# The second batch's attention denominators: repeating transfers through HBM in place of matmuls with a spreading matrix

## The chip, the cores and the metric

One core of a Trainium2 chip runs one program. The metric is device time in microseconds (us), lower is better. The program uses TensorE (PE in the profile; its weight loads are PEld), VectorE (DVE), ScalarE (ACT), GpSimd (POOL) and SyncE (SP), which issues almost all transfers. Everything is float32.

## What is computed

One transformer layer over 2 x 1024 tokens of width 512, on normalized input: linear attention with 16 heads of 32 features beside a gated feed-forward layer with low-rank experts. The part that the change touches is the division in the attention:

```python
Q = jax.nn.elu(Q) + 1.0
K = jax.nn.elu(K) + 1.0
KV = jnp.einsum('bhsd,bhse->bhde', K, V)
QKV = jnp.einsum('bhsd,bhde->bhse', Q, KV)
K_sum = jnp.sum(K, axis=-2)
QK_sum = jnp.einsum('bhsd,bhd->bhs', Q, K_sum)
out = QKV / (QK_sum[..., None] + 1e-08)
```

The kernel divides early: it multiplies each query feature by one over its head's denominator, so that `Q / denominator` can be stored and later be multiplied by `KV` and the output weights together. There is one denominator for each head and token, and 32 features of a head share it. After the attention and the experts the layer adds `x`.

## The kernel before

**Tiling and stages.** Tokens are two batches of 1024, each seen as two halves (`g` 0 and 1) of 512. Keys come first (`k_pair`), then the queries of batch 0 (`query_unit(0)`), its denominators (`denominators(0)`, line 874), the queries of batch 1 (`query_unit(1)`), its denominators, the leftover columns of the gate and up weights for both batches (`rest(0)` and `rest(1)`, line 1053), ten units of the feed-forward layer (`unit(j, b)`, line 1250), and the down projection. Products are split by Strassen's scheme, so between matmuls there are many sums of tokens, of weights and of results.

**Query features.** A batch has eight blocks of features, `qt[b, c, g]`, each 128 features (chunk `c`, four heads) by 512 tokens. Batch 0 has them in eight tiles of a work pool. Batch 1 has them in two slots: slot 4 holds the blocks of `c` 0 and 2, slot 5 those of `c` 1 and 3. Both slots are used again soon: slot 5 for `wi` (`inner_weight_sums`, line 1165, called at line 1491), slot 4 for `ti23_0` (`token_sums_23`, line 1149, called at line 1506).

**Denominators.** Eight matmuls a batch (line 879) gather them in one PSUM tile, 128 rows (four for each of 16 heads and two halves, equal among themselves) by 512 tokens; VectorE adds epsilon and takes the reciprocal into `den` (lines 883 and 884). A row then has to reach the 32 partitions of its head.

- Batch 0: `den` is stored to `d_dram` (line 887) and each block gets a tile `bc` by four transfers, each of which reads one row and writes it to 32 partitions (line 871, `spread_den`), 64 KB each. There are three `bc` buffers (`NBC`): a block's transfers are issued when an earlier multiply has freed one. `attend(0)` multiplies two blocks at a time, at four points of `query_unit(1)`.
- Batch 1: eight matmuls (line 901) with the 0/1 matrix `spread`, which GpSimd builds early (`make_spread`, line 220), put the repeated rows into PSUM banks `pb`. `attend(1, 0)` stands at the end of `rest(0)` and `attend(1, 1)` right after it.

In both, a multiply (line 909) works in place, and a transfer (line 914) stores the block to `q_dram`, 256 KB.

**Order.** On PE, DVE, ACT and POOL the order is the one in which the code calls the instructions. SyncE's order is made by a scheduler when the program is built, and then is fixed. Each engine works in its order and waits in place. Transfers use eight completion counters in turn, so each waits until the one issued eight before it has landed.

**What stands around.** On VectorE, from the reciprocal on: four sums `ti` (line 1135), two rows `hr` (line 1068, the gated product of `rest`), eight additions for the folding of low-rank weights (line 975), an `hr` row, the eight multiplies, eight weight sums of unit 0 (`fold_sums`, lines 979 to 982), four token sums (`token_sums_1`, line 1157), three `hr` rows, four sums `wi` (lines 1179 to 1182), two `hr` rows, and then the first unit. On GpSimd: `xdiff` (line 1013), eight weight sums `w` and `wi2` (line 1179), and without a break four `ti23_0`, four token sums of batch 1, four `ti56_1` and four `ti23_1` (lines 1135 and 1157); after these the two adds `r<-r,r` of the first unit (line 1365, by the helper's line 1287). In a unit, `r<-r,x` (line 1219) and `r<-r,ab` (lines 1233 and 1241) read PSUM halves that TensorE then writes again, and `r<-r,b` (line 1287, called at line 1378) overwrites the tiles that GpSimd's adds read.

```python
    def rest(b, between=(None, None)):        # line 1053
...
    rest(0, (first_fold, lambda: attend(1, 0)))
    attend(1, 1)
    token_diffs(1, "den")
    for i in range(2):
        fold_sums(0, i)
    token_sums_1(nc.vector, 0)
    rest(1, (lambda: list(inner_weight_sums(nc.vector, 0, (1, 5, 6))), None))
```

Of the kernel before, what the change touches and what calls it, by code (L numbers as in the profile page):

```python
# [10 lines left out]
F32 = mybir.dt.float32  # L11
# [4 lines left out]
P = 128  # L16
# [21 lines left out]
def layer_kernel(  # L38
# [23 lines left out]
    nc = tc.nc  # L62
# [26 lines left out]
    SG = P // 32  # L89
# [3 lines left out]
    NPQ = NC // 2  # L93
    WARM = 13, 3
    NBC = 3
# [20 lines left out]
    r_dram = [dram.tile([2, REST, 2, UT], F32, name=f"r_dram{b}") for b in range(NBATCH)]  # L116
    q_dram = [[dram.tile([2, P, 4, UT], F32, name=f"q_dram{b}_{j}") for j in range(NPQ)] for b in range(NBATCH)]
    w_dram = [dram.tile([E, 2 * TPB, P], F32, name=f"w_dram{b}") for b in range(NBATCH)]
    d_dram = dram.tile([P, TB], F32, name="d_dram")
    kvo_dram = [dram.tile([P, NC, D], F32, name=f"kvo_dram{b}") for b in range(NBATCH)]  # L120

    ffn_stack = ExitStack()
# [8 lines left out]
    p2 = pool(p2_stack, "p2")  # L131
    p2w = pool(p2_stack, "p2w", bufs=2)
# [6 lines left out]
    ident = const.tile([P, P], F32, name="ident")  # L139
# [5 lines left out]
    def hold(v):  # L145

        nc.vector.memset(v, 0.0)
# [48 lines left out]
    for b in range(NBATCH):  # L196
        t = p2.tile([P, 2, NC, 32], F32, name=f"ksd{b}")
# [16 lines left out]
    nc.gpsimd.memset(before, 0.0)  # L214
    for e in range(1, E):
        nc.gpsimd.memset(before[:, e, 0:e], 1.0)

    spread = p2.tile([P, 2, P], F32, name="spread")

    def make_spread():  # L220
        for c in range(SG):
            rows = slice(c * 32, (c + 1) * 32)
            for g in range(2):
                nc.gpsimd.tensor_copy(
                    spread[rows, g, :].rearrange("p (h k) -> p h k", k=DK),
                    ident[rows, :]
                    .rearrange("p (c h j) -> p c h j", h=HPC, j=32 // HPC)[:, c, :, 4 * g : 4 * g + 1]
                    .to_broadcast([32, HPC, DK]),
                )

    idle = p1.tile([P, 2], F32, name="idle")
    nc.gpsimd.memset(idle, 0.0)
    mv = p1.tile([P, NTILE, nc.vector.BN_AGGR_DIM], F32, name="mv")
# [442 lines left out]
    for n in range(2):  # L676
# [13 lines left out]
        (2, "n"): [load_factors],  # L690
        (2, "b"): [lambda: load_weights(wv_sb, wvT)],
        (3, "n"): [lambda: next(wq_sums)],
        (3, "b"): [lambda: load_weights(wo_sb, woT), gather_factors, make_spread],
        (4, "n"): [lambda: next(wq_sums), lambda: next(wq_sums)],
        (6, "n"): [lambda: next(wq_sums)],
        (7, "n"): [lambda: pair_token_sums(0)],
# [8 lines left out]
    def load_weights(t, w):  # L705
        hold(t[:, 0, 0:1])
        nc.sync.dma_start(out=t, in_=by_chunk(w))

    late = None
    for m in range(NTILE // 2):  # L710
# [21 lines left out]
        else:  # L732
# [4 lines left out]
            if m == 3:  # L737
                wo_sb = slot(5, [NC, D], "wo_sb")
# [118 lines left out]
            nc.tensor.matmul(pa, agu_sb[:, c, :], xt(b, c, cols), start=(c == 0), stop=(c == NC - 1))  # L857
        nc.vector.tensor_mul(xa[b][:, cols], pa, wT[b][:, cols])

    dens, bcs = {}, {}  # L860

    def spread_den():

        i = len(bcs)
        if i == 2 * NC:
            return
        g, c = divmod(i, NC)
        t = p2w.tile([P, TB], F32, tag=f"bc{i % NBC}", name=f"bc{i}", bufs=1)
        for h in range(HPC):
            row = c * 32 + 8 * h + 4 * g  # L870
            nc.sync.dma_start(out=t[h * DK : (h + 1) * DK, :], in_=d_dram[row, :].partition_broadcast(DK))
        bcs[i] = t

    def denominators(b):

        pd = bank(f"pd{b}")
        for g in range(2):
            for c in range(NC):
                nc.tensor.matmul(
                    pd[c * 32 : (c + 1) * 32, :], ksd[b][:, g, c, :], qt[b, c, g], start=(g == 0), stop=(g == 1)  # L880
                )
        den = ffn.tile([P, TB], F32, tag="den", name=f"den{b}")
        nc.vector.tensor_scalar_add(den, pd, DIV_EPS)
        nc.vector.reciprocal(den, den)
        dens[b] = den
        if b == 0:
            nc.sync.dma_start(out=d_dram, in_=den)
            for i in range(NBC):
                spread_den()

    attended = []

    def attend(b, g=None):

        if b:
            todo = [(c, g) for c in range(NC)]
            by = []
            for c in range(NC):
                rows = slice(c * 32, (c + 1) * 32)
                by.append(bank(f"pb{b}_{g}_{c}"))  # L900
                nc.tensor.matmul(by[c], spread[rows, g, :], dens[b][rows, :], start=True, stop=True)
        else:
            k = len(attended)
            attended.extend((k, k + 1))
            todo = [(i % NC, i // NC) for i in attended[-2:]]
            by = [bcs[i] for i in attended[-2:]]
        for (c, g), t in zip(todo, by):
            v = qt[b, c, g]
            nc.vector.tensor_mul(v, v, t)
            if b == 0:  # L910
                spread_den()

            j, i = c % NPQ, c // NPQ
            nc.sync.dma_start(
                out=q_dram[b][j][:, :, 2 * i + g, :].rearrange("s p n -> p s n"),
                in_=v.rearrange("p (s n) -> p s n", n=UT),
            )

# [134 lines left out]
    def rest(b, between=(None, None)):  # L1053
        t, _, bd = w_rest
        spare = [f"qt{k}{g}" for k in range(NC) for g in range(2)]
        blk = [ts(g, TB) for g in range(2)]

        def gated_rows(ps, first, n, g, dst):

            h, v = (  # L1060
                p2w.tile([P, TB], F32, tag=spare.pop(0), name=f"{n_}{b}_{g}_{dst.start}", bufs=1) for n_ in ("hr", "ur")
            )
            gr, ur = slice(first, first + n), slice(first + n, first + 2 * n)
            nc.scalar.activation(h[gr, :], ps[gr, :], AF.Silu)
# [12 lines left out]
        halves = [ps[2 * RB * g : 2 * RB * (g + 1), :] for g in range(2)]  # L1077
        for g in range(2):
            nc.tensor.matmul(halves[g], bd[:, P:], xa[b][:, blk[g]], start=True, stop=False, skip_group_check=True)
        for k in range(NC):  # L1080
            for g in range(2):
                nc.tensor.matmul(
                    halves[g], t[:, k, P:], xt(b, k, blk[g]), start=False, stop=(k == NC - 1), skip_group_check=True
                )
        flush()
        for g in range(2):
            gated_rows(ps, 2 * RB * g, RB, g, slice(RA, REST))
        for g in range(2):
            ps = bank(f"pr{b}_{g}")
            nc.tensor.matmul(ps, bd[:, 0:P], xa[b][:, blk[g]], start=True, stop=False)  # L1090
            for k in range(NC):
                nc.tensor.matmul(ps, t[:, k, 0:P], xt(b, k, blk[g]), start=False, stop=(k == NC - 1))  # L1092
            flush()
            gated_rows(ps, 0, RA, g, slice(0, RA))
            if between[g]:
                between[g]()
# [56 lines left out]
    def token_sums_1(eng, b):  # L1153

        t = xnT[b][0][:, :, TB:BT].rearrange("p k (h n) -> p k h n", n=TH)
        b11, b21 = tsum[b][1][:, 0], tsum[b][1][:, 1]
        eng.tensor_sub(t[:, 0, 0], b11[:, TH:], b11[:, 0:TH])
        eng.tensor_sub(t[:, 0, 1], b21[:, TH:], t[:, 0, 0])
        eng.tensor_sub(t[:, 1, 0], b21[:, TH:], b11[:, TH:])
        eng.tensor_sub(t[:, 1, 1], b21[:, 0:TH], t[:, 0, 1])  # L1160
        inner_tokens(b, (1,), lambda i, k: t[:, k // 2, k % 2])
# [320 lines left out]
        for i in range(2):  # L1482
            fold_adds(0, i, pf)

    rest(0, (first_fold, lambda: attend(1, 0)))
    attend(1, 1)
    token_diffs(1, "den")
    for i in range(2):
        fold_sums(0, i)
    token_sums_1(nc.vector, 0)  # L1490
    rest(1, (lambda: list(inner_weight_sums(nc.vector, 0, (1, 5, 6))), None))
    flush()
    ps8.close()
    p2_stack.close()
# [683 lines left out]
```

## Time and profile before

| | |
|---|---|
| median of three runs | 722.59 us (722.54 to 722.98) |
| the profiled execution's own time | 722.83 us |
| its span in the profile | 721.0 us, 9901 instructions |
| TensorE busy | 714.4 us (99%), 3426 matmuls |
| VectorE busy | 578.4 us (80%) |
| ScalarE, GpSimd busy | 198.3 us (28%), 142.6 us (20%) |
| `pb` matmuls (16 passes of 0.587 us, overlapping) | from 222.9 to 225.4 us |
| multiplies of batch 0, of batch 1 | 0.687 and 0.680 us each |
| `bc` transfers of batch 0 | 32, issued from 179.9 to 201.3 us |
| `TensorE` clock granted | 1.00 |

Times in the profile are counted from the start of its span. A row of a timeline gives the start, the time until the last of the row's instructions ends, the engine, the line, the operation, output and inputs by name, how many (`x8`), and in brackets how long the engine had been idle just before and what ended that. A matmul in float32 takes two or more passes, and so a row can say `x16` for eight matmuls. `SPq` rows are the issue of a transfer on SyncE, not its landing. The chain of waits gives start, length and what the path went through.

### The profile page before, as it was taken

The numbers are of one execution on the slowest core, as the hardware profiler recorded it, in microseconds if no ns is written. First come the engines' busy times: TensorE is split into PE (matmuls) and PEld (weight loads), VectorE is DVE, ScalarE is ACT, GpSimd is POOL, SyncE is SP. The second block draws the span as 40 slices with busy tenths as digits, with TensorE's granted clock in tenths as the row PEclk, the third lists the DMA queues.
The fourth block names the chain that finished last, engine by engine and source line by source line (L and its number), as shares of the span: only waits on it lengthen the run. The fifth ranks groups of instructions, "written<-read, shape, count | busy, mean of one in ns | idle before, by whom it ended". The sixth has DMA issues, their size and how long they took to land.

```text
span 721.0 us, 9901 instructions
## 1 busy us (share of the span) xinstructions
PE 714.4 (99%) x3426; PEld 491.4 (68%) x3426; DVE 578.4 (80%) x1327; ACT 198.3 (28%) x438; POOL 142.6 (20%) x176
## 2 busy tenths in 40 slices
PE   8999999999999999999999999999999999999998
PEld 6666676454434566566566566566688899899897
DVE  7788767777688678778778778878988889998884
ACT  3534413453532333333333333333200000000000
POOL 4033011101001752211211311544520100000000
PEclk9999999999999999999999999999999999999999
DMA  5243001214475101211211201334662444433101
GB/s 174 103 129 112 1 0 42 57 34 134 128 204 171 30 27 35 89 48 44 89 38 51 87 32 58 117 127 136 205 193 107 128 156 126 146 120 110 59 16 45
DMA packets 61734, 66.85 MB, mean 93 GB/s; under 512 B 10866, under 2 KB 49522, under 8 KB 61428
## 3 DMA queue, kind: packets, MB, share of 16 engines
q1 hardware_dynamic: 61154, 66.20, 29.9%
q8 instruction: 27, 0.44, 0.3%
q14 instruction: 23, 0.19, 0.1%
q10 hardware_dynamic: 530, 0.02, 0.0%
HBM read 44.11 MB, written 22.09 MB: 92 GB/s over the span
## 4 chain that ended last, share of the span: by engine, by line
PE 85%; DVE 12%; ACT 2%; issue 1%; POOL 0%; DVEq 0%; POOLq 0%
PE ab L1205 16%; PE b L1265 8%; PE po L1953 7%; PE pg L410 5%; PE pqu L778 4%; PE pya L1782 4%; PE pxa L1782 4%; PE pyb L1782 3%; PE ph L1650 3%; PE x L1205 3%; PE pxb L1782 2%; PE pyc L1782 2%; PE pxa L857 2%; PE b L1260 2%; PE pqv L778 2%; PE pr L1092 2%
## 5 line engine op out<-in xcount | busy, mean ns | idle before, releaser
L1265 PE MATMUL b<-t,w 128*128 128x512 f32 x160 | 83.2, 601 | 0.1
L410 PE MATMUL pg<-kt,xn 128*128 128x512 f32 x128 | 58.7, 594 | 0.5 <-DVE kt L354 0.5
L1287 POOL TENSOR_TENSOR r<-r,r 128x512 f32<-128x512 f32 x20 | 30.1, 1524 | 85.2 <-DVE t L1287 83.0
L1205 PE MATMUL ab<-ti,wi 128*128 128x256 f32 x180 | 45.4, 379 | 0.0
L1205 PEld LDWEIGHTS ab<-ti,w 128*128 128x128 f32 x140 | 25.1, 189 | 29.5 <-DVE r L1233 8.2
L1287 DVE TENSOR_TENSOR r<-r,r 128x512 f32<-128x512 f32 x60 | 43.2, 762 | 0.0
L1205 PEld LDWEIGHTS ab<-ti,wi 128*128 128x128 f32 x180 | 34.2, 190 | 13.2 <-issue 4.8
L1205 PE MATMUL ab<-ti,w 128*128 128x256 f32 x140 | 41.2, 387 | 0.5 <-DVE r L1233 0.2
L410 PEld LDWEIGHTS pg<-kt,xn 128*128 128x128 f32 x128 | 23.1, 190 | 22.6 <-issue 20.6
L1233 DVE TENSOR_TENSOR r<-r,ab 128x256 f32<-128x256 f32 x50 | 20.9, 419 | 21.6 <-ACT r L1230 21.1
L1238 ACT COPY r<-ab 128x256 f32<-128x256 f32 x50 | 18.6, 373 | 71.1 <-PE ab L1205 71.1
L1265 PEld LDWEIGHTS b<-t,w 128*128 128x128 f32 x160 | 29.2, 190 | 10.6 <-issue 5.9
L1241 DVE TENSOR_TENSOR r<-r,ab 128x256 f32<-128x256 f32 x50 | 20.9, 419 | 16.2 <-ACT r L1238 15.9
L1215 ACT COPY r<-ab 128x256 f32<-128x256 f32 x50 | 18.7, 374 | 48.4 <-PE ab L1205 47.1
L1953 PE MATMUL po<-wd,f 128*128 128x256 f32 x140 | 30.9, 380 | 0.1
L419 POOL TENSOR_TENSOR ksum<-ksum,kt 128x512 f32<-128x512 f32 x12 | 15.8, 1318 | 71.4 <-DVE lg L456 42.4
L1226 ACT COPY r<-ab 128x256 f32<-128x256 f32 x50 | 18.6, 373 | 40.7 <-PE ab L1205 40.7
L1896 DVE TENSOR_TENSOR f<-f 128x256 f32<-128x256 f32 x84 | 29.4, 423 | 0.1
L1953 PEld LDWEIGHTS po<-wd,f 128*128 128x128 f32 x140 | 26.4, 190 | 4.4 <-issue 0.9
L1205 PE MATMUL ab<-xnT,w 128*128 128x256 f32 x100 | 29.4, 390 | 0.0
L1205 PE MATMUL ab<-xnT,wi 128*128 128x256 f32 x100 | 28.1, 379 | 0.0
L1205 PEld LDWEIGHTS ab<-xnT,w 128*128 128x128 f32 x100 | 18.1, 189 | 10.9 <-issue 4.5
(483 smaller groups left out, 1652.1 us busy)
## 6 DMA issues: line engine op xcount, KB each, us to landing
h_dram<-h SPq DMA_DIRECT2D x40, 256.0 KB
f<-h_dram SPq DMA_DIRECT2D x10, 512.0 KB
x_ring<-in_x_dram SPq DMA_DIRECT2D x16, 256.0 KB
q_dram<-qt SPq DMA_DIRECT2D x16, 256.0 KB
xr<-in_x_dram SPq DMA_DIRECT2D x16, 256.0 KB
out_dram<-xr SPq DMA_DIRECT2D x15, 256.0 KB
w<-in_w_gate_dram SPq DMA_DIRECT2D x10, 256.0 KB
w<-in_w_up_dram SPq DMA_DIRECT2D x10, 256.0 KB
```

Source lines behind the costliest of these rows:

```text
L410: nc.tensor.matmul(pg[m], xns[n][:, ts(m, P)], kt, start=(j == 0), stop=(j == TPBATCH - 1))
L778: nc.tensor.matmul(banks[c], wqs[p][:, k, ts(c, P)], tsum[b][p][:, k, :], start=(start and k == 0), stop=(k == 1), skip_group_check=True,)
L1205: nc.tensor.matmul(out, w, t, start=start, stop=True, skip_group_check=True)
L1215: nc.scalar.copy(self.r[0][:, H0], self.ua)
L1233: nc.vector.tensor_add(self.r[1][:, H1], self.r[1][:, H1], self.lo)
L1241: nc.vector.tensor_add(self.r[1][:, H0], self.r[1][:, H0], self.lo)
L1265: nc.tensor.matmul(pb[m], ws[m][:, A_OF[p], ts(k, P)], tsum[b][p][:, k, :], start=start, stop=True, skip_group_check=True)
L1287: eng.tensor_add(to[m], t[m], v[m])
L1650: nc.tensor.matmul(phs[u][g * ER : (g + 1) * ER, :], a, f[:, g, :], start=(ns[0] == 0 and n == 0), stop=(last and n == len(chunks) - 1), s ...
L1782: nc.tensor.matmul(o, lhsT, rhs, start=first, stop=True, skip_group_check=True)
L1896: op(t[:, at, :], t[:, x_, :], t[:, y, :])
L1953: nc.tensor.matmul(ps[p][:, q, :], lhsT, rhs, start=start, stop=stop, skip_group_check=True)
```

## The change

Batch 1 gets its denominators as batch 0 does: `den` is stored to a `d_dram` of its own, and each block's `bc` tile comes by four repeating transfers. `spread`, `make_spread` and the eight matmuls into `pb` are gone. `CHUNKS` gives batch 1 an order of blocks of its own: the four of slot 5 (`c` 1 and 3, both halves), then the four of slot 4. `attend(1)` handles two blocks a call, at four places: two calls after the token sums that follow `rest(0)`, one in the middle of `rest(1)`, one at its end. `fold_sums` moves up into `rest(0)`, and the `wi` sums move from the first to the second place in `rest(1)`.

```diff
-    d_dram = dram.tile([P, TB], F32, name="d_dram")
+    d_dram = [dram.tile([P, TB], F32, name=f"d_dram{b}") for b in range(NBATCH)]
...
-        (3, "b"): [lambda: load_weights(wo_sb, woT), gather_factors, make_spread],
+        (3, "b"): [lambda: load_weights(wo_sb, woT), gather_factors],
...
-    dens, bcs = {}, {}
-    def spread_den():
-        i = len(bcs)
-        if i == 2 * NC:
-            return
-        g, c = divmod(i, NC)
-        t = p2w.tile([P, TB], F32, tag=f"bc{i % NBC}", name=f"bc{i}", bufs=1)
+    CHUNKS = [[(c, g) for g in range(2) for c in range(NC)], [(c, g) for j in (1, 0) for g in range(2) for c in (j, j + NPQ)]]
+    bcs = []
+    def spread_den(b, i):
+        if i >= 2 * NC:
+            return
+        c, g = CHUNKS[b][i]
+        t = p2w.tile([P, TB], F32, tag=f"bc{i % NBC}", name=f"bc{b}_{i}", bufs=1)
         for h in range(HPC):
             row = c * 32 + 8 * h + 4 * g
-            nc.sync.dma_start(out=t[h * DK : (h + 1) * DK, :], in_=d_dram[row, :].partition_broadcast(DK))
-        bcs[i] = t
+            nc.sync.dma_start(out=t[h * DK : (h + 1) * DK, :], in_=d_dram[b][row, :].partition_broadcast(DK))
+        bcs.append(t)
...
-        dens[b] = den
-        if b == 0:
-            nc.sync.dma_start(out=d_dram, in_=den)
-            for i in range(NBC):
-                spread_den()
+        nc.sync.dma_start(out=d_dram[b], in_=den)
+        attended.append(0)
+        for i in range(NBC):
+            spread_den(b, i)
...
-    def attend(b, g=None):
-        if b:
-            todo = [(c, g) for c in range(NC)]
-            by = []
-            for c in range(NC):
-                rows = slice(c * 32, (c + 1) * 32)
-                by.append(bank(f"pb{b}_{g}_{c}"))
-                nc.tensor.matmul(by[c], spread[rows, g, :], dens[b][rows, :], start=True, stop=True)
...
+    def attend(b):
+        for _ in range(2):
+            i = attended[b]
+            attended[b] += 1
+            c, g = CHUNKS[b][i]
             v = qt[b, c, g]
-            nc.vector.tensor_mul(v, v, t)
-            if b == 0:
-                spread_den()
+            nc.vector.tensor_mul(v, v, bcs.pop(0))
+            spread_den(b, i + NBC)
...
-    rest(0, (first_fold, lambda: attend(1, 0)))
-    attend(1, 1)
+    rest(0, (first_fold, lambda: [fold_sums(0, i) for i in range(2)]))
+    token_sums_1(nc.vector, 0)
+    attend(1)
+    attend(1)
     token_diffs(1, "den")
-    for i in range(2):
-        fold_sums(0, i)
-    token_sums_1(nc.vector, 0)
-    rest(1, (lambda: list(inner_weight_sums(nc.vector, 0, (1, 5, 6))), None))
+    rest(1, (lambda: attend(1), lambda: list(inner_weight_sums(nc.vector, 0, (1, 5, 6)))))
+    attend(1)
     flush()
```

In the built program this gives the following orders (blocks and their repeats numbered 0 to 7 in `CHUNKS[1]`).

- VectorE, after the folding additions and an `hr` row: eight weight sums, four token sums, multiplies 0 to 3, three `hr` rows, multiplies 4 and 5, an `hr` row, four `wi` sums, multiplies 6 and 7, an `hr` row, the first unit.
- SyncE, after the weight loads of units 0 and 1: the store of `den`, repeats 0 to 2, three stores to `r_dram`, repeat 3, store 0, repeat 4, store 1, repeat 5, store 2, repeat 6, store 3, three stores to `r_dram`, repeat 7, stores 4 and 5, a store to `r_dram`, stores 6 and 7, a store to `r_dram`, and then sixteen loads `sb`.
- TensorE: the same without `pb`. ScalarE: the same. GpSimd: the same without the eight copies of `make_spread`.
- Waits of the built program that concern this: repeat n (from 3 on) for multiply n - 3; the first `wi` for stores 0 to 3; `ti23_0` for stores 4 to 7; ScalarE's last `hr` row for the last of batch 0's stores to `r_dram`.

More of the change, by code (lines that the diff above doesn't have):

```diff
@@ L216, in layer_kernel @@
         nc.gpsimd.memset(before[:, e, 0:e], 1.0)
-    spread = p2.tile([P, 2, P], F32, name="spread")
-    def make_spread():
-        for c in range(SG):
-            rows = slice(c * 32, (c + 1) * 32)
[L223 to L229, printed above, removed]
     idle = p1.tile([P, 2], F32, name="idle")
@@ L884, in denominators @@
         nc.vector.reciprocal(den, den)
-        dens[b] = den
-        if b == 0:
-            nc.sync.dma_start(out=d_dram, in_=den)
-            for i in range(NBC):
-                spread_den()
-    attended = []
-    def attend(b, g=None):
-        if b:
-            todo = [(c, g) for c in range(NC)]
-            by = []
-            for c in range(NC):
-                rows = slice(c * 32, (c + 1) * 32)
-                by.append(bank(f"pb{b}_{g}_{c}"))
[L901 to L907, printed above, removed]
+        nc.sync.dma_start(out=d_dram[b], in_=den)
+        attended.append(0)
+        for i in range(NBC):
+            spread_den(b, i)
+    attended = []
+    def attend(b):
[3 more added lines that the diff above has]
+            c, g = CHUNKS[b][i]
             v = qt[b, c, g]
-            nc.vector.tensor_mul(v, v, t)
-            if b == 0:
-                spread_den()
-            j, i = c % NPQ, c // NPQ
+            nc.vector.tensor_mul(v, v, bcs.pop(0))
+            spread_den(b, i + NBC)
+            j, k = c % NPQ, c // NPQ
             nc.sync.dma_start(
-                out=q_dram[b][j][:, :, 2 * i + g, :].rearrange("s p n -> p s n"),
+                out=q_dram[b][j][:, :, 2 * k + g, :].rearrange("s p n -> p s n"),
                 in_=v.rearrange("p (s n) -> p s n", n=UT),
```

## The prediction

> All times are microseconds on the axis of the profiled run before. "Block n" (0 to 7) is the second batch's n-th piece of query features, "repeat n" the four transfers that bring its denominators, "multiply n" and "store n" its DVE instruction and its way to q_dram.
>
> **What bounds the kernel.** I read engine totals first (TensorE 714.4 of 721.0), then the chain of waits around the second batch's division, which gives what removing matmuls can be worth:
>
> ```profile
> 219.52 3.43 PE pr L1092 x8
> 222.96 2.41 PE pb L901 x15
> 225.36 1.01 PE pr L1079 x4
> ...
> 249.96 0.68 PE pf L966 x8
> 250.64 1.40 DVE w L975 x4
> ```
>
> From 195 to 250 the chain is matmuls alone, and pb stands in it with 2.41. So TensorE loses 2.41 of work, unless it then waits. Next the timelines of the engines that must follow. SyncE's queue and VectorE in the first batch, which already repeats through HBM:
>
> ```profile
> 177.85 0.35 SPq L887 DMA_DIRECT2D d_dram<-den  x1
> ...
> 179.94 11.17 SPq L871 DMA_DIRECT2D bc<-d_dram  x16
> 191.16 0.42 SPq L914 DMA_DIRECT2D q_dram<-qt  x1
> 191.69 1.80 SPq L871 DMA_DIRECT2D bc<-d_dram  x4
> 193.53 0.42 SPq L914 DMA_DIRECT2D q_dram<-qt  x1
> 194.26 1.69 SPq L871 DMA_DIRECT2D bc<-d_dram  x4
> ...
> 213.63 1.66 SPq L941 DMA_DIRECT2D w<-in_w_up_dram  x2
> ```
> ```profile
> 188.71 1.28 DVE L909 TENSOR_TENSOR qt<-qt,bc 128x512 f32<-128x512 f32 x2
> ...
> 199.56 0.69 DVE L909 TENSOR_TENSOR qt<-qt,bc 128x512 f32<-128x512 f32 x1 [1.28 <-DMA bc<-d_dram]
> ...
> 264.92 1.28 DVE L1287 TENSOR_TENSOR r<-r,b 128x512 f32<-128x512 f32 x2 [0.30 <-PE b L1260]
> 267.18 0.42 DVE L1241 TENSOR_TENSOR r<-r,ab 128x256 f32<-128x256 f32 x1 [0.97 <-ACT r L1238]
> ```
>
> A repeat costs SyncE 1.7 to 1.8, a store 0.42, and VectorE waited once, although the first batch had a whole query stage to hide in. GpSimd is the third to read:
>
> ```profile
> 240.22 1.71 POOL L1135 TENSOR_TENSOR ti<-xnT 128x512 f32<-128x512 f32 x1
> ...
> 258.30 1.28 POOL L1135 TENSOR_TENSOR ti<-xnT,ti 128x512 f32<-128x512 f32 x1
> 261.84 2.82 POOL L1287 TENSOR_TENSOR r<-r,r 128x512 f32<-128x512 f32 x2 [2.26 <-ACT h L1272]
> ```
>
> From 240.22 to 259.58 it works without a gap (16 instructions, 19.36), and only then comes to two adds that VectorE and TensorE need.
>
> **Part 1, removed.** The eight matmuls: -2.41. With them goes VectorE's wait of 2.23 for pb; there it now takes the sums that stood behind. The eight spread copies on GpSimd (0.28 each, at 55) lay in idle time: 0. The eight multiplies stay: 0.61 apart from PSUM (4.87 in all), 0.60 apart from SBUF (two in 1.28); 0.
>
> **Part 2, the first repeats.** Den's store stands on SyncE behind the weights of two units, so it issues at 215.3 to 215.65, behind 2 MB; DMA is busy until 219, and 256 KB more at the 290 GB/s seen there take 0.9. First repeat issue: 219.8. Twelve at 0.45 (179.94 to 185.36 held twelve): 225.2. That each transfer also waits for the one eight before it cost the first batch no pace, so none here. From last issue to release I need a duration. Bounds: den's own store took 1.74 (178.20 to 179.94) as the low end; repeat 3 of the first batch, issued by 191.12, was used at 194.15 (at most 3.0); repeat 5, issued by 195.95 with a store ahead of it, was awaited until 199.56 (3.6). I take 2.8 with nothing ahead and 3.3 with stores ahead. Repeats 0 to 2 are in at 224.4, 226.2, 228.0. VectorE, after the folding row that ends at 221.82, does eight weight sums (2.93) and four token sums (2.13): 226.9. Multiplies 0 to 2 run 226.9 to 228.8. So far hidden.
>
> **Part 3, the recycled repeats.** There are three buffers, so repeat 3 waits for multiply 0. It issues 0.71 after that starts (188.71 to 189.42), 227.6 to 229.3, and lands at 232.1: VectorE idles 3.3. SyncE is in order: store 0 to 229.8, repeat 4 to 231.7, store 1 to 232.1, repeat 5 to 234.0, store 2 to 234.5, repeat 6 to 236.4, store 3 to 236.8, three r_dram stores (1.73, as at 234.85) to 238.5, repeat 7 from 238.6 to 240.3. VectorE: multiply 3 and three hr rows (2.24) to 235.0; multiply 4 at 235.0, 5 at 237.3, an hr row to 238.6. The sums wi go into the slot that held blocks 0 to 3, so they wait for store 3, 2.0 after its issue (bounds 1.74, den's store, and 2.9, the store of an output tile at 600.95 whose tile was reloaded at 603.84; this queue is nearly empty): 238.8. The third sum is done 1.6 later, 240.4 (in the profile 237.79). TensorE, 2.41 early, wants it at 238.6 and waits 1.9. ScalarE, held by an r_dram store in the same stretch, gives its copy of the first product at about 240.7, so the two waits end together. Multiply 6 at 240.9, multiply 7 at 240.3 + 3.3 = 243.6. Then an hr row, two sums and the reading of a PSUM half that TensorE needs at 245.19 are over at 246.2: by here the gain is gone and TensorE is 1.0 late.
>
> **Part 4, GpSimd.** Its first ti of that row of sixteen overwrites blocks 4 to 7, so it waits for store 7: issue 0.71 after multiply 7 starts, 0.42 for itself, 2.0 to land, 246.7 instead of 240.22. The slack before the adds is 2.26. Queued behind it are sums that TensorE reads at 253.23 (the third ti, done by 251.0), 257.0 (the fourth, 252.2) and from 269.16 on (token sums, 255); these come in time. The adds don't: sixteen sums to 266.1, adds to 268.9 instead of 264.66. VectorE's second r<-r,b overwrites what the second add reads; it ends at 269.6, and the read of ab behind it (L1241) at 270.0 instead of 267.60. From there VectorE has no gap until 272.35, where TensorE takes up its bank within 0.1. So the delay passes on whole: **+2.4**. Later TensorE stays the bound and nothing in the trace is tied to a fixed time, so it stays.
>
> **Two rules against rows.** The rows give 3.3 for repeat 7. The Trainium skill (SBUF — State Buffer, "The DMA setup-cost knee") says about 2 plus bytes at 436 GB/s, 2.15 from the issue of 64 KB, an estimate of 1.75 after the issue ends. Then multiply 7 is 1.55 earlier and the sum +0.85. The awaited repeat 5 decides for the row. The same page, "Who interferes with whom", says that a VectorE instruction with two SBUF inputs and a GpSimd one that reads SBUF block each other. This trace shows ti sums of 1.27, and of 1.71 to 1.73 beside r<-r,r rows (two took 2.68 at 251.96, 1.29 elsewhere). Shifted sums meet other VectorE rows: by the rule some 1.3 more, by the row of sixteen as it stands 0. I take 0, and put the 1.3 into the range; undisturbed at 1.23 and 0.70 apart the sixteen would take 17.6, 1.8 less.
>
> **Sum.** -2.41 + 1.9 and 1.5 (waits in unit 0, batch 0) + 1.4 (wait at GpSimd's adds) = +2.4. Span 721.0 to 723.4; the profiled run's 722.83 becomes 725.2, and the median of 722.59 becomes **725.0**.
>
> **Rivals.** (a) Everything is hidden: repeats land before VectorE asks. The full 2.41 stays, 720.2. For it speaks that the first batch lost only one wait. Against it, SyncE alone needs 12.7 from the start of repeat 3 to the end of repeat 7, where VectorE, unhindered, is through in 9.8 (eight multiplies of 0.6, four hr rows of 2.9 together, four wi sums of 2.1). It decides from the point where multiply 7 starts by 241.2 (a gain of 1.45 at TensorE's wait for VectorE) and GpSimd's row starts by 242.8, or by 244.6 if it runs undisturbed. 0.11. (b) The GpSimd row runs faster or repeat 7 lands as the skill says: losses and gain cancel, within 0.2%, about 722.9. The low ends, -1.6 for repeat 7, -0.3 for store 7, -1.8 for GpSimd, are enough in part. 0.21. (c) The den store lands later behind the 2 MB (by 1 there is no cover left, beyond it everything shifts one to one), GpSimd is blocked more (1.3), store 7 takes 2.9: about +4.5, 727.1. 0.13. The forecast keeps 0.55. That the change doesn't do what it says is excluded: the built order has no pb and 33 transfers more.
>
> **Range.** A measurement here tells 0.2% (1.45) from no change. From (b)'s low end to most of (c): 722.0 to 727.0. Faster 0.11 from (a), same 0.21 from (b), slower 0.68 from forecast and (c).
>
> **What would show it.** Right: VectorE idle of about 3 before multiply 3 and 2 before multiply 7, both ended by bc; TensorE waiting at ab<-xnT,wi in the first unit; GpSimd's first ti near 246.7; a VectorE wait ended by GpSimd before r<-r,b. Wrong: multiplies without DMA waits, ti near 240, or the second unit's ab<-xnT,wi (269.16 in the profile) before 268.

## The result and the profile after

The kernel after takes **726.72 us** (median of four runs, 725.93 to 726.92), beside 722.57 for the kernel before in the same session (722.13 to 722.98): a ratio of 1.0053, 95% interval 1.0042 to 1.0065. The profiled execution took 726.92, its span is 725.1 (before: 721.0), so the trace has 4.1 to explain.

From the page of the kernel after: the engine totals, and the TensorE clock in 40 slices.

```profile
PE 714.0 (98%) x3410; PEld 491.5 (68%) x3410; DVE 581.1 (80%) x1327; ACT 198.0 (27%) x438; POOL 142.4 (20%) x168
...
PEclk9999999999999899999999999999999999999999
```

TensorE has 16 matmul records fewer and is busy for as long as before (714.4): what the eight matmuls took has come back as slower matmuls. One slice of the clock row reads 8.

The chain of waits, which held matmuls alone around the division before, now has this in it (start, length, what the path went through):

```profile
237.71 3.35 DMA r_dram<-hr
...
241.16 0.60 ACT hr L1040
...
242.38 0.38 ACT r L1191
...
242.80 4.64 PE ab L1181 x10
```

An `r_dram` store lands 3.35 after the start of its issue, ScalarE's last `hr` row was waiting for it (it overwrites the tile that the store reads), ScalarE's copy of the first product stands behind that row, and TensorE waits for the copy. Why the store is so late is in SyncE's queue, which is in order: it stands behind repeat 6 and store 3.

```profile
235.33 1.81 SPq L858 DMA_DIRECT2D bc<-d_dram  x4
237.18 0.42 SPq L890 DMA_DIRECT2D q_dram<-qt  x1
237.71 1.77 SPq L1045 DMA_DIRECT2D r_dram<-hr  x3
```

The timelines of VectorE, and then of TensorE, in the same stretch:

```profile
231.65 0.69 DVE L886 TENSOR_TENSOR qt<-qt,bc 128x512 f32<-128x512 f32 x1 [3.11 <-DMA bc<-d_dram]
...
237.06 0.69 DVE L886 TENSOR_TENSOR qt<-qt,bc 128x512 f32<-128x512 f32 x1 [2.10 <-DMA bc<-d_dram]
...
240.27 0.56 DVE L1155 TENSOR_TENSOR wi<-w 128x384 f32<-128x384 f32 x1 [1.92 <-DMA q_dram<-qt]
```
```profile
242.80 2.08 PE L1181 MATMUL ab<-xnT,wi 128*128 128x256 f32 x4 [4.46 <-ACT r L1191]
```

The same row of TensorE in the profile before:

```profile
241.01 1.03 PE L1205 MATMUL ab<-xnT,wi 128*128 128x256 f32 x4
```

VectorE waits for repeat 3 and repeat 5, and `wi` waits for store 3; its third sum is done at 241.9, so ScalarE's copy at 242.8 is the later of two waits that end nearly together. TensorE stands still for 4.46. Then a row of four matmuls takes 2.08, where before it took 1.03. The next view splits the time around the standstill into stretches of 3.41. Its columns are the stretch and its length, then busy time and number of instructions of PE, PEld, DVE, ACT and POOL, then the clock that TensorE was granted (1.00 is full speed), the busy share of the DMA engines, and GB/s:

```profile
237.58:241.00 3.42, 0.77 (x4) 0.34 (x2) 1.46 (x4) 0.00 (x0) 0.00 (x0) 1.00 0.84 224
241.00:244.41 3.41, 1.61 (x4) 1.34 (x5) 3.41 (x6) 1.82 (x4) 2.81 (x4) 0.50 0.72 230
244.41:247.82 3.41, 3.41 (x9) 2.53 (x8) 1.45 (x3) 1.09 (x3) 0.98 (x2) 0.50 0.75 224
247.82:251.24 3.42, 3.42 (x18) 1.94 (x17) 2.24 (x7) 0.77 (x3) 3.34 (x4) 1.00 0.08 12
```

From 241.00 to 247.82 TensorE's clock is exactly half. It works in 5.0 of these us, and loses 2.5.

**The account.** Up to the last matmul before the standstill TensorE is 2.83 earlier than before: 2.41 from the removed matmuls, and 0.42 by which this execution was ahead long before the change acts (it was 0.41 ahead at 134.5). The next one starts 1.79 later (242.80 for 241.01), a loss of 4.62 from start to start. From there to `ab<-xnT,w` takes 6.76 instead of 4.18, 2.58 more at half clock. So TensorE is 4.37 late at 249.56, 4.05 late at the second unit's first matmuls that read `wi` (273.21 for 269.16), and 4.1 late at the end.

### The profile page after: what moved, and what is told of

It reads as the page before. It is cut to its first block, busy times and chain, and to the rows that moved or that the text cites. A ratio compares the mean times of both kernels' runs of the same rounds, so it can differ in the third digit from the quotient of the medians.

```text
span 725.1 us, 9908 instructions
## 1 busy us (share of the span) xinstructions
PE 714.0 (98%) x3410; PEld 491.5 (68%) x3410; DVE 581.1 (80%) x1327; ACT 198.0 (27%) x438; POOL 142.4 (20%) x168
## 4 chain that ended last, share of the span: by engine, by line
PE 77%; DVE 14%; DMA 4%; ACT 2%; issue 2%; SPq 1%; DVEq 0%; ACTq 0%
PE ab L1181 16%; PE b L1241 8%; PE po L1929 7%; PE pg L396 5%; PE pya L1758 4%; PE pxa L1758 3%; PE pqu L764 3%; PE pyb L1758 3%; PE ph L1626 3%; PE x L1181 3%; PE pxb L1758 2%; PE pyc L1758 2%; PE b L1236 2%; PE kua L425 2%; DMA bc<-d_dram 1%
## 5 line engine op out<-in xcount | busy, mean ns | idle before, releaser
L1181 PE MATMUL ab<-xnT,wi 128*128 128x256 f32 x100 | 29.6, 396 | 4.5 <-ACT r L1191 4.5
```

The source lines that it names most:

```text
L1181: nc.tensor.matmul(out, w, t, start=start, stop=True, skip_group_check=True)
```

## The experiments

The theory after reading this: the removal is worth its 2.41; against it stand one standstill of 4.5 (it ends with ScalarE's copy; `wi` was ready 0.9 before), and the half clock that follows it. Rivals: the slow matmuls come from something else (transfers, VectorE and GpSimd traffic); the new order on VectorE costs the time, not the repeats; three buffers are too few; GpSimd's late row costs what the prediction gave it. All ratios below are to the kernel before in the same session (722.57 to 722.65).

### The clock: work in the gap, and gaps of chosen length

**Filling the gap, first try.** In unit 0, ahead of the first matmul that reads `wi`:

```diff
+        if (j, b) == (0, 0):
+            fill = held("fill", 0)
+            for _ in range(5):
+                nc.tensor.matmul(fill, ident, xt(0, 0, slice(0, TB)), start=True, stop=True)
         i1.b()
```

> The kernel after, with five extra 128x512 matmuls of TensorE (identity by normalized tokens, into a PSUM bank that is not in use, result never read) between the last first-product matmul of unit 0, batch 0, and the first one that reads wi; the output stays the reference's. A pair of 128x512 passes takes 0.86 us in this stretch, so the five fill about 4.3 of the 4.46 us in which TensorE stood still, and put nothing on the path. Theory (the stall itself is one loss, and a second one of about 2.5 us is the half clock that TensorE is granted for 5.0 us after it, because it had stood still): the clock stays at 1.0 through 242 to 250 us, ab<-xnT,wi takes 1.03 instead of 2.08, and the time falls from 726.7 by about 2.5 to 724.2. Rival (the slow matmuls come from something else that happens in that stretch, such as transfers or VectorE and GpSimd traffic): the matmuls stay slow, 726.7 +- 0.5.

Measured 730.9 (1.0109, 1.0094 to 1.0125): a miss, by the choice of PSUM bank. It was the one that ScalarE's last `ur` copy reads, so the extra matmuls waited for that copy as well, until 242.13, and came behind the standstill. They took 7.21 instead of 4.45, and the matmuls of unit 0 behind them ran at full speed (`ab<-xnT,wi` 1.03). So what is slow is whatever TensorE does first after standing still. That supports the theory but is not its test.

**Filling it in a free bank** (`held("fill", 1)`):

> As the run with five extra matmuls, but into a PSUM bank whose last reader is long done, so that they start when TensorE would stand still (238.3) and not after the standstill. Theory (the half clock comes from a stretch in which TensorE was mostly idle): no stretch at half clock, ab<-xnT,wi at 1.03, and TensorE 2.5 earlier at 250. For the total there are two cases. If nothing else is late, 726.7 - 2.5 = 724.2. If GpSimd's row of sixteen, which starts at 247.1 after store 7 and reaches its two adds at 267.0, is now what is late (it was hidden because TensorE was late too), the adds end at 269.9 instead of 270.5 and the total falls by only 0.6 to 1.0: about 725.9. I expect the second. Rival (the slow matmuls have another cause): slow rows stay, 726.7.

TensorE's timeline of this kernel:

```profile
237.78 4.45 PE L1282 MATMUL fill<-xnT,ident 128*128 128x512 f32 x10
242.07 1.03 PE L1181 MATMUL ab<-xnT,wi 128*128 128x256 f32 x4
```

No standstill, no slow row, clock 1.0 throughout. The mean clock of all five executions is 0.999 or 1.000, where those of the kernel after have 0.995 three times (two stretches at half clock) and 0.998 once (one stretch). Nothing in transfers, VectorE or GpSimd was changed, so the slow matmuls are due to the standstill. Measured 726.1 (1.0047, 1.0034 to 1.0059), where 725.9 was expected: the 2.5 are won in unit 0, but at the end only 0.6 is left of it, which is within the spread of the runs. The section on GpSimd's row shows where the rest went.

**A standstill in the kernel before**, made by repeating ScalarE's last `ur` copy, with nothing else of the change:

```diff
-            nc.scalar.copy(v[gr, :], ps[ur, :])
+            for _ in range(10 if (b, g, first) == (1, 1, 0) and n == RA else 1):
+                nc.scalar.copy(v[gr, :], ps[ur, :])
```

> The kernel before (with the matmuls into pb), with ScalarE's last ur copy of rest(1) made nine times more, 0.60 us each, so that the copy that TensorE waits for comes 5.4 later: a stall of about 4.6 us at the same matmul as in the kernel after, and no other part of the change. Theory (a standstill of this length halves TensorE's clock for about 5 us): stall 4.6 plus 2.5, 722.6 + 7.1 = 729.7, with a granted clock of 0.5 in the rows after the stall. Rival (the slow matmuls belong to the repeats and their traffic, not to the standstill): 722.6 + 4.6 = 727.2, clock 1.0.

Measured 729.87 (1.0098, 1.0084 to 1.0112): a standstill of 4.63, and the clock halved for 3.41 after it. Its stretches of 3.41:

```profile
240.53:243.94 3.41, 1.71 (x6) 0.77 (x5) 0.00 (x0) 3.25 (x6) 3.33 (x5) 1.00 0.18 38
243.94:247.35 3.41, 0.48 (x2) 0.46 (x3) 0.90 (x1) 3.00 (x7) 3.33 (x4) 1.00 0.00 0
247.35:250.77 3.42, 3.42 (x9) 2.72 (x9) 0.86 (x3) 0.74 (x2) 3.37 (x4) 0.50 0.18 38
```

The stretch from 241.01 to 245.19 in the profile before took 1.79 longer here. That sums to 6.4 of the 7.5 between the two spans; the other 1.07 was there already at 136.0, long before the repeated copies, so it belongs to this execution and not to the standstill.

**A shorter standstill**, with five extra copies in place of nine:

> As the run with a long stall, but five extra copies: a stall of about 2.2 us. Theory (only a standstill longer than some 3 us costs clock; the forecast's own stalls of 1.9 had none): 722.6 + 2.2 = 724.8, clock 1.0. Rival (any standstill costs clock in proportion to its length): 722.6 + 2.2 + 1.2 = 726.0 and slow rows after it.

Measured 725.13 (1.0035, 1.0022 to 1.0048; 724.47 to 726.36). The profiled execution was the one of 726.36. Its stretches of 3.41:

```profile
240.93:244.34 3.41, 1.24 (x7) 1.06 (x7) 1.60 (x2) 2.37 (x6) 3.33 (x4) 1.00 0.00 0
244.34:247.76 3.42, 3.42 (x8) 2.35 (x7) 1.13 (x4) 1.10 (x3) 3.34 (x5) 0.50 0.18 38
```

In this execution a standstill of 2.17 was enough, and cost 1.80 of slow matmuls. So my theory of a limit at some 3 us does not hold, and neither does the rival's proportion: 2.17 cost 1.80, and 4.63 cost 1.79. But the other four executions of this kernel (724.47 to 725.37) have a mean clock of 1.000, where one stretch at half clock gives 0.998, as in the profiled one. By that number they paid the standstill alone, and so did the median: 725.13, where the theory had 724.8.

What the traces show is a clock that is set for 3.41 at a time, by how busy TensorE was in the 3.41 before. TensorE's busy time in such a stretch, over the runs, and what came next: up to 1.39 (0.77 in the kernel after, 1.24 here, 1.39 in the first filled gap): half clock; 1.71 (twice: the long standstill and the run with six buffers below, each in its first stretch): no change. So in these traces the limit lies between 41% and 50%. The clock went back after a stretch with 2.79 or more busy, not after one with 1.61 or 1.96 at half clock. The Trainium skill (TensorE: Matmul & The Clock Gate, Part 1, "What's actually happening") describes such a free-running window of 3413 ns; the length agrees with these traces. Its table in "Why this matters for your kernels" warns of gaps above about 3 us; in the profiled execution here 2.17 was enough. There the standstill lies whole within one stretch (240.93 to 244.34). That in the other four it was divided between two stretches is likely, but was only argued: one execution was traced.

### GpSimd's row: the loss behind the loss

On GpSimd, added to the filled gap:

```diff
-    list(token_sums_23(0, slot(4, [2, 4, TH], "ti23_0")))
     token_sums_1(nc.gpsimd, 1)
+    list(token_sums_23(0, slot(4, [2, 4, TH], "ti23_0")))
```

> As the run before, and on GpSimd the four token sums of batch 1, which wait for no store, stand ahead of the four ti sums that wait for store 7. GpSimd then works through 2.4 us in which it waited. Theory (GpSimd's row is the second loss, hidden behind the first): adds end about 2.4 earlier than in the run before, and the full 2.5 of the clock shows: 724.2 to 724.4. Rival (GpSimd's row never mattered): the same time as the run without the swap.

Measured **724.55** (1.0024, 1.0015 to 1.0034). First the row of the kernel after that matters, GpSimd's first `ti`:

```profile
247.09 1.27 POOL L1111 TENSOR_TENSOR ti<-xnT 128x512 f32<-128x512 f32 x1 [2.43 <-DMA q_dram<-qt]
```

Then VectorE and TensorE in the run with the filled gap alone, and VectorE with GpSimd's swap added:

```profile
263.85 3.11 DVE L1263 TENSOR_TENSOR t<-t,r 128x512 f32<-128x512 f32 x2
267.68 0.70 PE L1181 MATMUL ab<-ti,w 128*128 128x256 f32 x2 [0.90 <-DVE r L1209]
```
```profile
264.71 2.02 DVE L1263 TENSOR_TENSOR t<-t,r 128x512 f32<-128x512 f32 x2
```

In the kernel after, TensorE is 4.4 late when GpSimd's row comes in, and it waits for nothing from there to the second unit, so the row delays it no further. As soon as TensorE is 2.5 earlier, the row takes the place of the clock and keeps most of it; with token sums in the 2.43 in which GpSimd waited for store 7, another 1.55 shows. The traces say by which path. From unit 0's first `ab<-xnT,wi` to the second unit's, TensorE takes 28.15 before, 29.32 with the gap filled and 28.25 with the swap added. The wait for GpSimd's adds is not what differs: VectorE waits for them at `r<-r,b` for 0.49 and 0.54 without the swap, and for 0.38 and 0.54 with it. What differs is VectorE beside GpSimd's row: two additions `t<-t,r` took 3.11, 2.02 with the swap, and 1.29 in the profile before, where that row was over. An `r<-r,ab` behind them comes late, and TensorE waits 0.90 for it. (One execution of each kernel was traced.)

What is left, 724.55 - 722.64 = 1.9, is the standstill less the matmuls, 4.46 - 2.41 = 2.05. That closes the account: clock and GpSimd overlap and are together worth 726.72 - 724.55 = 2.2.

### What TensorE waits for

**ScalarE's tiles.** `hr` and `ur` of the last group in two free tiles:

```diff
         spare = [f"qt{k}{g}" for k in range(NC) for g in range(2)]
+        if b:
+            spare[6:] = ["tmp", "tmp"]
...
```

> The kernel after, with the last pair of hr and ur tiles of rest(1) in two other free tiles, so that ScalarE's last hr row no longer waits for an r_dram store of batch 0 that SyncE issues among the repeats. Theory (two waits end together, ScalarE's copy at 242.8 and the wi sums at 241.9): ScalarE goes on at about 236, TensorE waits for VectorE's third wi alone, until about 241.9, so the stall shrinks by only 0.9, from 4.46 to 3.6; with the clock still dropping 725.8, without a drop (if 3.6 is too short for one) 723.3. Rival (the ScalarE wait alone is the cost, and wi is in time): the stall goes to under 1, 720.5 to 721.5.

TensorE's timeline of this run:

```profile
241.97 2.05 PE L1183 MATMUL ab<-xnT,wi 128*128 128x256 f32 x4 [3.15 <-DVE wi L1159]
...
248.10 0.73 PE L1183 MATMUL ab<-xnT,wi 128*128 128x256 f32 x2 [2.56 <-ACT r L1204]
```

ScalarE went on at 236.28, and TensorE then waited for the third `wi` sum until 241.97, as the theory had it: the second wait stands right behind the first. But the time was 732.43 (1.0136, 1.0117 to 1.0154), where 725.8 was expected. The new tiles lie where unit 0 puts its first results, and ScalarE's copy into those waited 8.72 for the last `r_dram` store. A second standstill of 2.56, and a second stretch at half clock, came of that.

**The order alone.** Matmuls into `pb` as before, but blocks and places as in the change:

```diff
-            todo = [(c, g) for c in range(NC)]
+            todo = [(c, g) for j in (1, 0) for g in range(2) for c in (j, j + NPQ)][2 * g : 2 * g + 2]
...
+    attend(1, 0)
     attend(1, 1)
...
+    rest(1, (lambda: attend(1, 2), lambda: list(inner_weight_sums(nc.vector, 0, (1, 5, 6)))))
+    attend(1, 3)
```

> The kernel before, with its eight matmuls into pb and no transfers, but with everything else of the change: blocks in the new order, two blocks at each of the four new places, fold_sums and token sums ahead of them, the wi sums at the second place of rest(1). Theory (the repeats cost the time, the order costs nothing): stores 0 to 3 go out at once, wi and the r_dram store are in time, TensorE keeps its 2.41 of matmuls: 722.6 +- 0.5. Rival (the new order on VectorE makes wi and the multiplies late by itself): 724 or more, with a stall at ab<-xnT,wi.

Measured 724.89 (1.0033, 1.0020 to 1.0045), by the number the rival's. The timelines of TensorE, VectorE and GpSimd say why:

```profile
222.46 1.99 PE L901 MATMUL pb<-den,spread 32*128 32x512 f32 x8
...
236.27 0.54 DVE L1179 TENSOR_TENSOR wi<-w 128x384 f32<-128x384 f32 x1
...
240.10 1.28 POOL L1013 TENSOR_TENSOR xdiff<-xa 128x512 f32<-128x512 f32 x1 [62.34 <-PE pb L901]
```

The first four matmuls hold TensorE for 1.91 (to its next row at 224.37), the two later pairs for 1.05 and for 1.36, the latter with a wait of 0.23: 4.3 together, against 2.41 for all eight in the profile before. This is 1.9 of the 2.2 lost. (In the profile before, four matmuls in a row use four different groups of 32 rows of `den`, here two; that this is the reason was only argued.) GpSimd's `xdiff` overwrites `den`, which the last pair reads, and so its whole row is late too. `wi` starts at 236.27, as before (236.17), without a wait. So VectorE's order does not by itself make `wi` late, but this kernel is not the order and nothing else; how much the order would cost with none of the matmuls changed stays open.

### What makes store 3 late

**One transfer for each repeat** of batch 1 (four rows to 32 partitions each, in one instruction), without and with GpSimd's swap:

```diff
+        if b:
+            rows = d_dram[b][c * 32 + 4 * g : c * 32 + 32 : 8, :]
+            nc.sync.dma_start(out=t, in_=rows.unsqueeze(1).to_broadcast([HPC, DK, TB]))
+        else:
...
```

> The kernel after, with each repeat of batch 1 as one transfer (four rows, each written to 32 partitions) instead of four, so that SyncE issues 8 instead of 32. Theory (SyncE's issue time of 1.8 a repeat is what makes repeats, store 3 and the r_dram store late): SyncE needs about 0.5 a repeat, multiply 3 may wait until about 231, multiplies 4 to 7 and the wi sums do not wait, ScalarE goes on at 236.3, TensorE does not stand still in unit 0; what is left is GpSimd, whose first ti comes at about 244.3 with store 7, so the adds end at about 267.3 instead of 270.5: about 723.4. Rival (the landing of 2.9 to 3.1 is the bound, not the issue): stalls at multiplies 3 and 5 and at wi shrink by a third at most, the clock still drops, about 725.5.

> The run with one transfer a repeat, and GpSimd's token sums of batch 1 ahead of the sums that wait for store 7. Theory: both losses go, and most of the 2.41 of the removed matmuls is left: 720.5 to 721.3, below the kernel before (722.6). Rival (GpSimd's row doesn't matter): no difference to the run without the swap.

Measured 733.31 (1.0149, 1.0135 to 1.0162) and 734.88 (1.0161, 1.0145 to 1.0178), some 10 and 14 above what was expected; TensorE stood still for 10.67 and 10.48. The first of the two runs: SyncE did issue a repeat in 0.53, but repeat 3, issued at 231.09, was awaited until 236.37, and repeats 4 and 5 came in 3.3 apart behind it. Busy time in a stretch, with the DMA share in the column before the last:

```profile
230.00:234.00 4.00, 4.00 (x10) 1.72 (x10) 0.00 (x0) 2.62 (x5) 0.00 (x0) 1.00 0.29 86
```

A share of 0.29 of the sixteen DMA engines is busy, the work of under five of them; in the four us before it was 0.21. The Trainium skill (DMA: Bandwidth & Descriptors, "Rules for kernel authors") says that a transfer whose outermost dimension is less than 16 is confined to as many engines; it is 4 here. This fits, but no run tried another shape. The scheduler also put eight `sb` loads ahead of repeat 3, which held SyncE until 231.0. So these two kernels say nothing for or against SyncE's issue time.

**Six buffers, one queue.** Three further `bc` tiles, the waiting `hr` row ahead of the multiplies, GpSimd's swap:

```diff
-        t = p2w.tile([P, TB], F32, tag=f"bc{i % NBC}", name=f"bc{b}_{i}", bufs=1)
+        t = p2w.tile([P, TB], F32, tag="tmp" if b and i % 6 >= NBC else f"bc{i % NBC}", name=f"bc{b}_{i}", bufs=3 if b and i % 6 >= NBC else 1)
...
     token_sums_1(nc.vector, 0)
+    flush()
     attend(1)
```

> The kernel after, with six bc buffers for batch 1 instead of three, the waiting hr row of rest(0) put ahead of the multiplies (so that its r_dram store is early and ScalarE is not held), and GpSimd's token sums ahead of the sums that wait for store 7. All repeats are still issued by SyncE. Theory (SyncE's issue time is the bound: with 24 transfers up to 230 and the stores behind repeats 6 and 7, store 3 goes out at about 238 and wi starts at 241): multiplies 3 to 5 come earlier, but TensorE still stands still for about 4 in unit 0 and its clock still drops: 725.5 +- 1. Rival (three buffers were the bound): no stall, 720.5 to 721.5.

Measured 729.06 (1.0097, 1.0082 to 1.0113). SyncE's issue and VectorE's `wi` in this run:

```profile
218.44 12.27 SPq L858 DMA_DIRECT2D bc<-d_dram  x24
...
237.54 1.49 SPq L890 DMA_DIRECT2D q_dram<-qt  x3
```
```profile
242.13 0.56 DVE L1155 TENSOR_TENSOR wi<-w 128x384 f32<-128x384 f32 x1 [4.49 <-DMA r_dram<-hr]
```

Four multiplies now run in a row from 227.45 to 229.93 without a wait for a repeat, so the buffers do what they should. But their stores stand behind 24 and then eight more transfers, store 3, the last of the row of three, goes out at about 238.6, and `wi`, which waits for it (the profile names an `r_dram` store that was issued right behind), starts 1.9 later than in the kernel after. Nor was ScalarE freed: its `hr` row at 232.60 had waited 8.63 for an `r_dram` store behind the 24 transfers. So three buffers alone were not the bound. The size was off: TensorE stood still for 5.74, not 4, and 725.5 was expected.

**Two queues.** Repeats 2 and 3 issued by ScalarE after its last copy of `rest(0)`:

```diff
-        for i in range(2 * NBC if b else NBC):
+        for i in (0, 1, 4, 5) if b else range(NBC):
...
+    for i in (2, 3):
+        spread_den(1, i, nc.scalar)
```

> As the run with six buffers, but repeats 2 and 3 (eight of the 32 transfers) are issued by ScalarE after its last copy of rest(0), where it has nothing to do for 3.6 us; SyncE keeps repeats 0, 1, 4, 5, 6, 7. Theory (SyncE's issue time is the bound): SyncE is 3.6 earlier from there on, store 3 goes out at about 233.5 and lands at 236.5, wi is done at about 238.5 where TensorE wants it at 238.3, no standstill over 0.5 and no drop of the clock; GpSimd's first ti at about 243.5 with its token sums already done, so that its adds are at most 0.6 late: 720.5 to 721.3, below the kernel before. Rival (landing times or GpSimd decide): 723 or more.

Measured 725.86 (1.0049, 1.0037 to 1.0062): 3.2 faster than with one queue, and far from the 720.5 to 721.3 expected. SyncE's sixteen transfers took 9.04 (0.57 each, against 0.51 above) and ScalarE's last six 4.52 (0.75 each), so all 24 were issued in 9.5 instead of 12.27: a second queue gave under a third more pace, not twice. Store 3 still went out at about 237.5, TensorE stood still for 3.37, and its clock halved for 3.41. So the queue's issue time is part of the cost. But the number is the rival's (723 or more, if landing times or GpSimd decide), and landing was not ruled out: from 238.78 to 242.19 the DMA engines are busy throughout (share 1.00, 309 GB/s), and `wi` starts 2.7 after the issue of store 3 ends. How much of the standstill is issue and how much landing, no run here separates.

**Half of the blocks.** The kernel before, with its first four blocks by matmuls, the other four by repeats into four buffers:

```diff
+    LAST = [(c, 1) for c in (1, 3, 0, 2)]
...
+        for i in range(NC if b else NBC):
+            spread_den(b)
...
+        if b and g:
+            todo = LAST
+            by = [bcs[2 * NC + i] for i in range(NC)]
+        elif b:
             todo = [(c, g) for c in range(NC)]
```

> The kernel before, with the change for half of the blocks only: the four of the first token half still get their denominators from matmuls into pb[...], the four of the second half by repeats, those of slot 5 first, into four bc buffers, so that no repeat waits for a multiply. VectorE's and GpSimd's orders stay as before. Theory (what cost the time was SyncE's issue time, 1.8 a repeat, ahead of store 3, and the recycling behind it): sixteen repeating transfers are issued by about 226.5, stores by 231, wi and GpSimd's ti wait for none; TensorE loses half of the 2.41, so 722.6 - 1.2 = 721.4. Rival (any transfers of denominators in this stretch cost more than the matmuls that they replace): 722.6 or more, with a wait for bc or for a store ahead of wi.

Measured 722.92 (1.0007, 1.0000 to 1.0013): no gain where 721.4 was expected, and by its number and its wait for `bc` the rival's. The timelines of VectorE, and then of TensorE:

```profile
229.56 0.69 DVE L914 TENSOR_TENSOR qt<-qt,bc 128x512 f32<-128x512 f32 x1 [1.31 <-DMA bc<-d_dram]
```
```profile
222.81 1.14 PE L906 MATMUL pb<-den,spread 32*128 32x512 f32 x8
...
240.00 0.70 PE L1210 MATMUL ab<-t,w 128*128 128x256 f32 x2 [1.11 <-ACT ur L1070]
```

The matmuls are 1.34 shorter, as planned. But the fourth repeat keeps VectorE waiting for 1.31, VectorE has no gap behind it, and its `hr` rows come at 235.22 instead of 233.89. The first of them goes to `r_dram`, by a store that SyncE issues at 236.18. By the built order ScalarE's last `hr` row waits for such a store, and it starts at 238.76 (the profile names a `wi` sum of VectorE that ended 0.1 before, so that it was the store is argued). TensorE then waits 1.11 for a bank that ScalarE reads. VectorE is 1.33 late, about as much as TensorE is early. No kernel tried here is faster than the one before.

## Why the prediction was right, and where it was off

The forecast was 725.0, slower, by +2.4; it is slower by 4.15, inside the range. The main mechanism was right: transfers that are recycled and queued on SyncE make `wi` and ScalarE late, and TensorE, 2.41 early, waits for them. That the sum came as near as it did is in part luck: two of its terms, 2.9 together, did not come, and losses that it did not have or had too small came to 5.3. By its steps:

- **Part 1** (-2.41): right. Less the 0.42 by which this execution was ahead anyway, TensorE is 2.41 earlier up to the standstill.
- **Part 2** (three repeats hidden): right. Multiplies 0 to 2 run without a wait at 226.39 (226.9 forecast).
- **Part 3** (recycled repeats): the repeats were timed within 0.5 (multiply 3 at 231.65 for 232.1, multiply 5 at 237.06 for 237.3). Mis-sized is store 3. Its issue ended at 237.60, not 236.8 (store 0 alone took 1.37 to issue, where 0.42 was taken), and it landed 2.7 later, where I took 2.0 because "this queue is nearly empty". So `wi` came 1.5 later and ScalarE's copy, forecast at 240.7, at 242.8. TensorE waits 4.46 where the forecast had 1.9.
- **The missed term**: the forecast had no loss of clock. It measures 2.58. Whether its own wait of 1.9 would have cost clock is open: one of 2.17 did so in one execution of five.
- **The wait of 1.5 for multiply 7** did not come: with TensorE late, multiplies 6 and 7 (242.54) had nothing to wait for.
- **Part 4** (+1.4 at GpSimd's adds): its start was right (`ti` at 247.09 for 246.7), and so were VectorE's waits for GpSimd at `r<-r,b` (0.39 and 0.54). But in the kernel itself it adds nothing, since TensorE is 4.4 late anyway. When TensorE's 2.5 of clock are won back, GpSimd's row keeps 1.2 of them in the trace and about 1.5 by the medians, and by another path than the adds: VectorE's additions beside it take longer. The forecast weighed such meetings as a longer GpSimd row only (0 in the sum, 1.3 in the range; it became 0.6 longer), not as slower VectorE rows.
- **The rules weighed**: for the last transfers of repeats 3 and 5 the chain shows 2.86 and 2.69 from the start of issue to landing, more than the 2.15 that the prediction worked out from the setup-cost rule. So the row of the first batch was the better guide.

Rival (a), all hidden, is refuted by the two waits for `bc`. Rival (b) let GpSimd's row run in 17.6, and it took 19.9; its early landing of repeat 7 was not put to the test, as nothing waited for it. Rival (c), 727.1, is nearest by its number, but of its causes the late `den` store was not there (the first repeats went out at 219.41, forecast 219.8), GpSimd was blocked 0.6 more and not 1.3, and store 7 landed 2.4 after its issue and not 2.9.

So the sum was -2.41 + 1.9 + 1.5 + 1.4. It is -2.41 + 4.6 + 2.6 = 4.8 with GpSimd's row under it; of this the trace has 0.3 won back by the second unit and 0.4 from the earlier start, which leaves the 4.1.

## What to carry to other kernels

A wait on the engine that bounds the kernel has two prices, its length and the clock after it; in these traces a stretch of 3.41 us with 1.4 or less of matmuls in it was followed by one at half clock, which cost about 1.8 where TensorE was busy throughout it. Whether a short wait meets this depends on where it falls: 2.2 us did so in one execution of five. When work is moved from TensorE to transfers, count the issue time of the queue, the stores that stand behind it and their landing, before counting buffers. And a loss that is hidden under a larger one is still there: taking away 2.5 of clock gave some 0.6, within the spread of the runs, until GpSimd's row was moved too.

## What the runs showed that was not expected

- A standstill of 2.17 us in one traced execution halved TensorE's clock for 3.41, as one of 4.63 did; with 4.46 in the kernel after it was 6.82, two stretches.
- Stores of 256 and 128 KB took 3.1 and 3.35 from the start of issue to release beside repeating transfers, where `den`'s first store took 2.1 in the profile before.
- Two issuing queues took 9.5 for 24 repeating transfers where one took 12.27, with a single one slower on each (0.57 on SyncE, 0.75 on ScalarE, for 0.51).
- The same eight matmuls of 32 rows held TensorE for 2.41 in one order and for 4.1 in another.
- Two additions of VectorE took 3.11 beside GpSimd's row of sums, and 1.29 where that row was over.
